# Summing a state-space scan by accumulating DMAs into a channel-major SBUF tile in place of transposes accumulated in PSUM

## The chip, the cores and the metric

The program runs on one core of a Trainium2 chip. Its engines are named as in the profile: PE (TensorE matmul), PEld (its weight loads), DVE (VectorE), ACT (ScalarE), POOL (GpSimd) and SP (SyncE, which here only issues DMAs). The metric is the device time of one execution in microseconds. Three runs of the kernel before gave 1719.56, 1720.71 and 1730.47 us, a median of 1720.71 us. The profiled execution took 1715.39 us, of which 1713.5 us lie between its first and its last instruction (the span).

## The reference

Two layers are computed on an input `x` of shape (2, 2048, 256), float32. The first is a Mamba block with a feed-forward part, multiplied by the SiLU of a second feed-forward part with weights and activations quantized to FP4; the second is an attention over the two batch entries, multiplied by the SiLU of a three-block network with quantized weights. The change touches the Mamba block alone:

```python
xz = x @ in_proj_w
xi, z = jnp.split(xz, 2, axis=-1)                    # 512 channels each
xc = silu(causal_conv4(xi) + conv_b)
dt, Bm, Cm = jnp.split(xc @ x_proj_w, [16, 32], axis=-1)
dt = softplus(dt @ dt_proj_w + dt_proj_b)
A = -jnp.exp(A_log)                                  # (512, 16)
def step(h, inp):
    dt_t, B_t, C_t, x_t = inp
    dA = jnp.exp(dt_t[..., None] * A)
    h = dA * h + dt_t[..., None] * B_t[:, None, :] * x_t[..., None]
    y = jnp.sum(h * C_t[:, None, :], axis=-1)        # the sum over the 16 states
    return (h, y)
y = ys + D * xc
y = y * silu(z)
return y @ out_proj_w
```

## The kernel before

The 2048 positions are cut into 16 units of 128 positions. One unit holds both batch entries, so 256 columns (`T`), and the 512 channels lie as four groups of 128 partitions (`m`). A unit has five stages: HEAD (norm, input projection, convolution, `dt`), QUANT (the FP4 feed-forward), SCAN, TAIL (the feed-forward after the Mamba block) and SECOND (the whole second layer). HEAD of unit u+1 is recorded ahead of the rest of unit u, and SECOND of a unit runs beside the scan of later units.

Nothing is issued where the code stands. A `Recorder` keeps every engine call, and `issue` puts them out in an order that a planner works out beforehand from costs written in `cost`, from data dependences and from free buffers, with hand-set numbers (`lead`, `bonus`, `adjust`, `passes`). The order on each engine's queue is then fixed, and an engine takes its queue strictly in order. All instructions therefore have the helper's line, L579, in the profile, and are told apart by the tiles that they write and read. The pools' buffer counts are fixed too: `hh`, `bcs` and `decay` have two buffers each, `xc` and `ux` one.

The scan (L982 to L1063) goes over the 16 states two at a time, so eight steps per unit and 128 steps in all. For one step:

- SP loads `bcs` (L997): B and C of the two states, copied to all 128 partitions, 512 KB.
- ACT writes `decay`, the exponentials, in eight instructions (L1001), and copies the state carried from the unit before into column 0 of `hh` (L1014).
- DVE multiplies `ux` by B into `hh` (L1017, "the first product"), scans `hh` with `decay` in place (L1019), and multiplies `hh` by C in place (L1027, "the second product"). Each is over 2048 columns.
- SP saves the last column of the scan in `state` (L1023), between the scan and the second product.
- PE transposes the 16 blocks of 128x128 of `hh` and accumulates them in two PSUM banks `y`, position-major (L1031). That is the sum over the states. It begins, per unit, with `D * xc` as eight matmuls against the diagonal `ddiag` (L989).

After eight steps `z` is projected position-major, its SiLU `sz` is multiplied with `y` (L1048), the product is transposed back to channel-major by PE and copied out of PSUM by ACT (L1051, L1053), and eight matmuls with `w_out` give `x2` (L1062). A buffer of `hh` is free for the first product of the next step but one when PE has transposed it.

The eight PSUM banks are shared out in `BANKS` (L30): two for `y`, two for `m` (HEAD and the end of SCAN), two for `f`, one each for `s` and `h`. POOL has little to do: the inverse square roots of the norms (`ln_y`, `ln_sq`, about six per unit).

Of the kernel before, what the change touches and what calls it, by code (L numbers as in the profile page):

```python
# [17 lines left out]
P = 128  # L18
D = 256
# [10 lines left out]
BANKS = {"y": 2, "m": 2, "f": 2, "s": 1, "h": 1}  # L30
USES = {
    "q": "f", "s0": "s", "s1": "s", "h0": "h", "h1": "h",
    "e0": "m", "e1": "y", "g0": "h", "g1": "f",
# [8 lines left out]
class Recorder:  # L42
# [69 lines left out]
    def cost(self, engine, method, args, kwargs):  # L112
# [6 lines left out]
        if engine == "gpsimd":  # L119
            if method == "memset":  # L120
                return 0.04
            return 0.69 if method == "tensor_tensor" else 0.19
# [88 lines left out]
    def prepare(self):  # L211
# [12 lines left out]
        for i, (engine, method, args, kwargs, stage) in enumerate(ops):  # L224
# [14 lines left out]
            if engine == "gpsimd":  # L239
                self.table[i] = int(method != "memset")  # L240
            if engine == "sync":
                self.size[i] = 2 if args[0].dtype == BF16 else 4
                for d in args[0].shape:
                    self.size[i] *= d
# [44 lines left out]
    def backward(self, unit, bonus, ahead):  # L289
# [7 lines left out]
        def transfer(i):  # L297
            return size[i] / self.RATE if engine[i] == "sync" else 0.0
# [68 lines left out]
    def forward(self, key, bonus, ahead):  # L367
# [65 lines left out]
        while done < n:  # L433
# [54 lines left out]
            if best_e == "sync":  # L488

                moved = max(moved, t + cost) + self.size[i] / self.RATE  # L490
                stop = moved + tails["sync"]
# [91 lines left out]
def tile_two_layers(ctx: ExitStack, tc: tile.TileContext, a: dict):  # L583
# [53 lines left out]
    def load_x(u):  # L637
        t = io.tile([P, B, D], F32, tag="xt", name=f"xt_{u}")
        rec.sync.dma_start(t, x[:, u * P : (u + 1) * P, :].rearrange("b p d -> p b d"))
        return t  # L640
# [72 lines left out]
    ddiag = const.tile([P, 4, P], F32, name="ddiag")  # L713
    for m in range(4):
        rec.vector.tensor_scalar(ddiag[:, m, :], ident, dvec[:, m : m + 1], None, ALU.mult)
# [145 lines left out]
    def make_qlora_weights():  # L861

        scl = load("q_scl", [P, 6, 2, D // BLK], a["scales"].rearrange("i (c p) n -> p i c n", p=P))
        wl = const.tile([P, 6, 2, D], F32, tag="w_l", name="w_l")
        for i in range(6):
            qi = tmp.tile([P, 2, D], I32, tag="t2k_s0", name=f"qi_{i}", bufs=depth["s0"])
            rec.sync.dma_start(qi, a["qweights"][i].rearrange("(c p) d -> p c d", p=P))
            lab = t2k("s0", f"lab_{i}")
# [5 lines left out]
            for c in range(2):  # L874
                wv = w[:, c, :].rearrange("p (n k) -> p n k", k=BLK)
                rec.vector.tensor_tensor(
                    wv, wv, scl[:, i, c, :].unsqueeze(2).to_broadcast([P, D // BLK, BLK]), ALU.mult
                )
# [103 lines left out]
    def scan(u, h):  # L982
# [3 lines left out]
        y = [bank("y", f"y_{nm}_{g}") for g in range(TG)]  # L986
        for g in range(TG):
            for m in range(4):
                rec.tensor.matmul(  # L989
                    y[g][:, m * P : (m + 1) * P], lhsT=h["xc"][:, m, g * P : (g + 1) * P],  # L990
                    rhs=ddiag[:, m, :], start=(m == 0), stop=False, skip_group_check=True,
                )
        bcv = h["bc"].rearrange("(s n) t -> s n t", s=2)
        for n in range(0, NS, 2):
# [32 lines left out]
            rec.vector.tensor_tensor(hv[:, :, :P], hv[:, :, 1:], cn, ALU.mult)  # L1027
            for k in range(2):
                for g in range(TG):
                    for m in range(4):  # L1030
                        rec.tensor.matmul(  # L1031
                            y[g][:, m * P : (m + 1) * P],
                            lhsT=hh[:, k, m, g, :P],
                            rhs=ident, is_transpose=True, start=False, stop=(n + k == NS - 1),
                            skip_group_check=True,
                        )

        y2 = [None] * TG
        for g in range(TG):
            pz = bank("m", f"pz_{nm}_{g}")  # L1040
            for c in range(2):
                rec.tensor.matmul(
                    pz, lhsT=h["lnt"][:, c, g * P : (g + 1) * P], rhs=w_in[:, c, DI : 2 * DI],
                    start=(c == 0), stop=(c == 1),
                )
            sz = scn.tile([P, DI], F32, tag="sz", name=f"sz_{nm}_{g}", bufs=1)
            rec.scalar.activation(sz, pz, AF.Silu)
            rec.vector.tensor_tensor(sz, y[g], sz, ALU.mult)  # L1048
            pt = bank("m", f"py_{nm}_{g}").rearrange("p (m t) -> p m t", m=4)
            for m in range(4):  # L1050
                rec.tensor.transpose(pt[:, m, :], sz[:, m * P : (m + 1) * P], ident)  # L1051
            y2[g] = t2k("m", f"y2_{nm}_{g}").rearrange("p (m t) -> p m t", m=4)
            rec.scalar.copy(y2[g], pt)  # L1053
        po = bank("m", f"po_{nm}").rearrange("p (g d) -> p g d", g=TG)
        for g in range(TG):
            for m in range(4):
                rec.tensor.matmul(
                    po[:, g, :], lhsT=y2[g][:, m, :],
# [255 lines left out]
    for u in range(NU):  # L1314
# [9 lines left out]
        x1 = mam.tile([P, B, D], F32, tag="x1", name=f"x1_{u}")  # L1324
        tail(u, h, x2, sgs, x1)
        rec.stage = (u, SECOND)
        if u == 0:
# [6 lines left out]
        (3, 1, 2.23), (9, 3, -0.03), (15, 4, 1.53), (5, 1, -1.64), (13, 0, 0.68), (14, 4, -2.53),  # L1334
        (3, 3, -0.31), (14, 1, 0.96), (6, 2, -0.01), (11, 4, 1.22), (14, 2, 1), (11, 1, 0.05),
        (8, 0, 0.01), (2, 1, -2.41), (13, 1, 2.14), (3, 2, 0.51), (6, 3, 1.05), (0, 1, 1.16),
        (11, 0, -0.47), (5, 3, -1.29), (14, 0, 0.2), (13, 4, -0.85), (7, 2, 0.99), (12, 1, 0.89),
        (13, 3, -0.99), (1, 2, 0.28), (15, 1, 2.77), (14, 3, -1.39), (8, 1, 0.09), (7, 3, -0.25),
        (15, 3, 1.61), (6, 1, 0.87),
    ]  # L1340
    passes = [
        (20.0, 0.3, 0.0, 1.02, 0.1, [
            (9, 4, -0.033), (9, 1, 0.008), (4, 2, "gpsimd", -0.309), (1, 3, "tensor", 0.016),
            (2, 1, "gpsimd", 0.015), (1, 4, "vector", -0.12), (7, 3, "scalar", -0.018),
            (7, 3, "vector", 0.085), (1, 2, "gpsimd", 0.027), (1, 1, "gpsimd", -0.003),
            (9, 4, "gpsimd", 0.128), (11, 1, "vector", -0.088), (3, 4, "gpsimd", -0.076),
            (15, 4, "vector", 0.027), (1, 2, "scalar", -0.075), (8, 0, "vector", 0.016),
            (15, 3, "scalar", -0.469), (7, 3, -0.043), (13, 0, "vector", -0.017),
            (4, 3, "gpsimd", -0.036), (6, 4, 0.029), (8, 2, "vector", 0.849),
            (7, 0, "vector", -0.277), (9, 1, "vector", 0.009), (8, 2, "gpsimd", -0.192),  # L1350
            (1, 3, "gpsimd", -0.014), (0, 0, -0.03), (1, 1, "scalar", -0.005), (15, 2, 0.008),
            (3, 2, "scalar", 0.081), (7, 4, 0.045), (8, 3, 0.119), (2, 0, "tensor", -0.001),
            (11, 4, -0.015), (6, 3, -0.002), (1, 3, "vector", -0.002),
        ]),
        (10.0, 0.5, 0.02, 0.7, 0.1, [
            (11, 1, -0.102), (2, 4, "scalar", 0.011), (5, 4, "vector", -0.034), (15, 4, -0.012),
            (1, 1, "gpsimd", -0.001), (0, 2, "scalar", 0.062), (6, 1, 0.102),
            (15, 3, "tensor", -0.001), (8, 0, "gpsimd", 0.078), (14, 3, "gpsimd", -0.002),
            (2, 3, "gpsimd", 0.073), (15, 0, "vector", 0.003), (11, 4, "gpsimd", -0.513),
            (8, 3, "scalar", 0.034), (6, 2, "vector", -0.182), (1, 0, "tensor", -0.047),  # L1360
            (13, 3, -0.126), (13, 1, "tensor", 0.078), (13, 0, 0.075), (9, 3, "scalar", 0.327),
            (13, 4, "scalar", -0.038), (10, 3, "gpsimd", 0.04), (7, 0, -0.033), (5, 4, -0.02),
            (11, 0, "gpsimd", 0.001), (12, 2, "vector", 0.022), (7, 3, "tensor", 0.011),
            (14, 3, "scalar", -0.562), (5, 1, 0.02), (11, 2, "vector", -0.033),
            (4, 4, "tensor", -0.007), (14, 2, "gpsimd", 0.082), (7, 4, -0.619),
            (12, 4, "gpsimd", -0.108), (0, 0, "vector", 0.038), (7, 0, "gpsimd", 0.595),
            (3, 0, "tensor", -0.063), (10, 1, "gpsimd", -0.034), (10, 3, "scalar", -0.054),
        ]),
        (20.0, 0.3, 0.12, 0.2, 0.12, [
            (11, 0, -0.044), (2, 3, 0.079), (0, 3, "scalar", -0.007), (5, 0, "tensor", 0.001),  # L1370
            (12, 2, "vector", -0.004), (9, 1, "scalar", -0.003), (7, 2, "gpsimd", 0.03),
            (6, 1, "scalar", 0.003), (11, 0, "gpsimd", 0.036), (10, 2, "gpsimd", -0.008),
            (12, 4, "gpsimd", -0.078), (15, 1, "tensor", 0.002), (7, 4, "vector", 0.006),
            (12, 0, -0.001), (10, 4, "tensor", 0.001), (4, 0, "vector", 0.015),
            (1, 0, "scalar", 0.054), (7, 0, -0.019), (12, 0, "gpsimd", 0.131),
            (1, 3, "gpsimd", 0.007), (8, 4, 0.054), (5, 1, "tensor", 0.032),
            (1, 1, "gpsimd", 0.061), (4, 2, "gpsimd", 0.387), (4, 4, -0.231),
            (7, 1, "scalar", 0.028), (12, 2, "gpsimd", 0.017), (8, 1, "tensor", 0.007),
            (8, 0, "tensor", 0.003), (3, 3, -0.006), (13, 0, "tensor", -0.004),
            (2, 3, "gpsimd", -0.063), (3, 4, "scalar", -0.014),  # L1380
        ]),
        (110.0, 0.3, 0.08, 0.206, 0.02, [
# [154 lines left out]
```

## Time and profile before

| | us |
|---|---|
| three runs, median (lowest, highest) | 1720.71 (1719.56, 1730.47) |
| profiled execution, whole | 1715.39 |
| its span, first to last instruction | 1713.5 |
| DVE busy | 1614.3 (94%), 1638 instructions |
| PE busy | 1552.3 (91%) |
| ACT busy | 1419.4 (83%), of it 313 table loads 401.6 |
| POOL busy | 183.5 (11%) |
| DMA engines | 25.5% of 16 engines, 86.36 MB on SP's queue |

The busy times by stretch are read as follows: from 100 to 1600 us DVE stands still for some 26 us in all (it is busy for 1474.0 us of them); the rest of its idle time is at the ends, 11.6 us in the first 100 us and 61.5 us after 1600 us. After 1616 us, when the last second product is over, the last unit's TAIL and SECOND run as one dependent chain that PE carries.

One unit is some 98 us long. Its eight steps take 8 x (2.28 + 4.45 + 2.28) us of DVE by the rows' means, and the rest of DVE's unit is the FP4 quantization, the norms and the gates.

### The profile page before, as it was taken

How to read it: one execution, taken by the hardware profiler on the slowest of the kernel's cores; microseconds unless marked ns; L12 is line 12 of the kernel's file. 1: busy time of each engine (PE TensorE's matmuls, PEld its weight loads, DVE VectorE, ACT ScalarE, POOL GpSimd, SP SyncE). 2: the span in 40 equal slices, each digit the busy share in tenths (PEclk: the TensorE clock that was granted, in tenths of full speed). 3: DMA queues.
4: the chain of work that ended last, by engine and by line, in shares of the span. 5: the costliest groups of instructions: out<-in, count | busy, mean ns of one | idle time of the engine just before them, and what ended most of it. 6: DMA issues, size and time to landing. Idle time of an engine off the chain costs nothing.

```text
span 1713.5 us, 21982 instructions
## 1 busy us (share of the span) xinstructions
PE 1552.3 (91%) x7948; PEld 1224.1 (71%) x7948; DVE 1614.3 (94%) x1638; ACT 1419.4 (83%) x2885; POOL 183.5 (11%) x114
## 2 busy tenths in 40 slices
PE   7736989999899999989999998999989899998997
PEld 5535758678687867768687876878677686867775
DVE  8999999999999999999999999999998999999932
ACT  5636877989899899899989898999978898897734
POOL 0000002001011201020102011001130101100100
PEclk9858989999999999999999999999999999999999
DMA  7322222313222232222222331222222132211000
GB/s 188 92 46 51 50 46 46 61 32 57 57 46 47 47 63 38 44 58 50 53 47 47 57 58 32 51 64 38 57 44 46 44 51 51 51 44 50 25 7 13
DMA packets 310666, 87.75 MB, mean 51 GB/s; under 512 B 262775, under 2 KB 276765, under 8 KB 310558
## 3 DMA queue, kind: packets, MB, share of 16 engines
q1 hardware_dynamic: 310558, 86.36, 25.5%
q8 instruction: 62, 1.02, 0.2%
q14 instruction: 46, 0.38, 0.1%
HBM read 80.62 MB, written 4.72 MB: 50 GB/s over the span
## 4 chain that ended last, share of the span: by engine, by line
PE 41%; ACT 20%; DVE 9%; issue 3%; POOL 1%; DMA 0%; POOLq 0%; ACTq 0%; SPq 0%; DVEq 0%
PE bank_f L579 16%; PE bank_m L579 8%; PE bank_s L579 7%; ACT decay L579 7%; PE bank_y L579 6%; ACT L579 6%; DVE hh L579 4%; ACT t2k_s L579 3%; PE bank_h L579 2%; DVE fp_l L579 2%; ACT t2k_f L579 1%; DVE t2k_s L579 1%; ACT dt L579 1%; POOL ln_sq_s L579 1%; ACT fp_h L579 0%
## 5 line engine op out<-in xcount | busy, mean ns | idle before, releaser
L579 DVE TENSOR_TENSOR_SCAN hh<-decay,hh 128x2064 f32<-128x2064 f32 x128 | 569.7, 4451 | 1.4 <-DVE ln_m_m L579 0.4
L579 ACT ACTIVATE decay<-dt,amat 128x256 f32<-128x256 f32 x1024 | 437.5, 500 | 34.3 <-DVE hh L579 33.0
L579 ACT ACT_TABLE_LOAD x313 | 401.6, 1283 | 16.5 <-DVE hh L579 3.9
L579 PE MATMUL bank_y<-ident,hh 128*128 128x128 f32 x2048 | 279.8, 283 | 36.1 <-DVE hh L579 36.1
L579 PEld LDWEIGHTS bank_y<-ident,hh 128*128 128x128 f32 x2048 | 246.6, 147 | 72.1 <-issue 47.1
L579 DVE TENSOR_TENSOR hh<-ux,bcs 128x2048 f32<-128x2048 f32 x128 | 291.8, 2279 | 6.7 <-PE bank_y L579 6.5
L579 DVE TENSOR_TENSOR hh<-hh,bcs 128x2048 f32<-128x2048 f32 x128 | 291.9, 2281 | 0.1
L579 POOL TENSOR_TENSOR ln_sq_s<-ln_sq_s,power 128x2 f32<-128x2 f32 x45 | 86.9, 1932 | 755.2 <-ACT ln_sq_s L579 755.2
L579 PE MATMUL bank_f<-w_f,t2k_f 128*128 128x256 f32 x512 | 133.6, 388 | 11.4 <-ACT t2k_f L579 11.3
L579 PE MATMUL bank_f<-t2k_f,w_f 128*128 128x256 f32 x512 | 127.6, 389 | 4.0 <-ACT t2k_f L579 3.3
L579 PE MATMUL bank_m<-xi,cdiag 128*128 128x256 f32 x512 | 124.8, 378 | 0.0
L579 PEld LDWEIGHTS bank_f<-w_f,t2k_f 128*128 128x128 f32 x512 | 94.3, 193 | 30.7 <-ACT t2k_f L579 17.6
L579 PEld LDWEIGHTS bank_f<-t2k_f,w_f 128*128 128x128 f32 x512 | 97.8, 194 | 21.7 <-ACT t2k_f L579 6.2
L579 PEld LDWEIGHTS bank_m<-xi,cdiag 128*128 128x128 f32 x512 | 93.6, 189 | 14.2 <-issue 0.5
L579 PE MATMUL bank_h<-t2k_s,w_l 128*128 128x256 f32 x360 | 92.0, 390 | 8.6 <-ACT t2k_s L579 8.6
L579 PE MATMUL bank_f<-w_down,hq 128*128 128x256 f32 x384 | 93.1, 386 | 6.7 <-ACT hq L579 6.5
L579 DVE SCALAR_TENSOR_TENSOR fp_l<-fp_h,fp_l 128x704 f32<-128x704 f32 (+2 forms) x124 | 91.8, 740 | 6.8 <-ACT fp_h L579 6.4
L579 PE MATMUL bank_f<-w_up,t2k_f 128*128 128x352 f32 x256 | 91.4, 475 | 6.0 <-ACT sg L579 2.9
L579 PE MATMUL bank_s<-w_qkv,t2k_s 128*128 128x256 f32 (+1 forms) x300 | 90.8, 430 | 4.1 <-DVE t2k_s L579 4.1
L579 PE MATMUL bank_f<-w_gate,t2k_f 128*128 128x352 f32 x256 | 90.0, 471 | 2.0 <-ACT h L579 2.0
L579 PE MATMUL bank_s<-w_l,t2k_s 128*128 128x256 f32 x360 | 89.3, 381 | 0.6 <-ACT t2k_s L579 0.6
L579 PEld LDWEIGHTS bank_f<-w_down,hq 128*128 128x128 f32 x384 | 71.6, 192 | 22.3 <-ACT hq L579 11.5
(172 smaller groups left out, 2434.2 us busy)
## 6 DMA issues: line engine op xcount, KB each, us to landing
bcs<-bc SPq DMA_DIRECT2D x128, 512.0 KB, 4.9
xt<-in_x_dram SPq DMA_DIRECT2D x16, 256.0 KB, 3.8
out_dram<-t2k_s SPq DMA_DIRECT2D x15, 256.0 KB, 2.2
w_f<-in_ffn_w_dram SPq DMA_DIRECT2D x2, 1024.0 KB
state<-hh SPq DMA_DIRECT2D x120, 8.0 KB, 2.9
t2k_s<-in_qweights_dram SPq DMA_DIRECT2D x6, 256.0 KB, 3.1
w_in<-in_in_proj_w_dram SPq DMA_DIRECT2D x1, 1024.0 KB, 5.1
h<-in_w_gate_dram SPq DMA_DIRECT2D x6, 128.0 KB
```

Of the source, the lines that this page charges most:

```text
L579: getattr(getattr(self.nc, engine), method)(*args, **kwargs)
```

## The change

The diff, with the planner's hand-set numbers (`adjust`, `passes`, `lead`, `bonus`) left out; all of those are new.

```diff
-BANKS = {"y": 2, "m": 2, "f": 2, "s": 1, "h": 1}
+BANKS = {"m": 3, "f": 2, "s": 2, "h": 1}
...
-    "e0": "m", "e1": "y", "g0": "h", "g1": "f",
+    "e0": "m", "e1": "m", "g0": "h", "g1": "f",
...
         if engine == "gpsimd":
+            if method == "dma_start":
+                return 1.1
...
-        t = io.tile([P, B, D], F32, tag="xt", name=f"xt_{u}")
+        t = io.tile([P, B, D], F32, tag="xt", name=f"xt_{u}", bufs=4)
...
-    ddiag = const.tile([P, 4, P], F32, name="ddiag")
-    for m in range(4):
-        rec.vector.tensor_scalar(ddiag[:, m, :], ident, dvec[:, m : m + 1], None, ALU.mult)
...
-        scl = load("q_scl", [P, 6, 2, D // BLK], ...)
         for i in range(6):
...
+            scl = small.tile([P, 2, D // BLK], F32, tag="q_scl", name=f"scl_{i}", bufs=2)
+            rec.sync.dma_start(scl, ...)
...
-        y = [bank("y", f"y_{nm}_{g}") for g in range(TG)]
-        for g in range(TG):
-            for m in range(4):
-                rec.tensor.matmul(
-                    y[g][:, m * P : (m + 1) * P], lhsT=h["xc"][:, m, g * P : (g + 1) * P],
-                    rhs=ddiag[:, m, :], start=(m == 0), stop=False, skip_group_check=True,
-                )
+        y = mam.tile([P, 2, 4, T], F32, tag="y", name=f"y_{nm}", bufs=1)
+        yv = y.rearrange("p k m (b t) -> p (k m b) t", b=B)
+        xc = h["xc"]
+        for m in range(4):
+            rec.scalar.activation(xc[:, m, :], xc[:, m, :], AF.Copy, scale=dvec[:, m : m + 1])
...
-            rec.vector.tensor_tensor(hv[:, :, :P], hv[:, :, 1:], cn, ALU.mult)
-            for k in range(2):
-                for g in range(TG):
-                    for m in range(4):
-                        rec.tensor.matmul(
-                            y[g][:, m * P : (m + 1) * P],
-                            lhsT=hh[:, k, m, g, :P],
-                            rhs=ident, is_transpose=True, start=False, stop=(n + k == NS - 1),
-                            skip_group_check=True,
-                        )
+            if n == 0:
+                rec.vector.tensor_tensor(yv, hv[:, :, 1:], cn, ALU.mult)
+                rec.gpsimd.dma_start(y[:, 0], xc, accum_op=ALU.add)
+            else:
+                rec.vector.tensor_tensor(hv[:, :, :P], hv[:, :, 1:], cn, ALU.mult)
+                rec.gpsimd.dma_start(yv, hv[:, :, :P], accum_op=ALU.add)
+        rec.gpsimd.dma_start(y[:, 0], y[:, 1], accum_op=ALU.add)
...
-            sz = scn.tile([P, DI], F32, tag="sz", name=f"sz_{nm}_{g}", bufs=1)
+            sz = scn.tile([P, 2, T], F32, tag="sz", name=f"sz_{nm}_{pr}", bufs=1)
             rec.scalar.activation(sz, pz, AF.Silu)
-            rec.vector.tensor_tensor(sz, y[g], sz, ALU.mult)
-            pt = bank("m", f"py_{nm}_{g}").rearrange("p (m t) -> p m t", m=4)
-            for m in range(4):
-                rec.tensor.transpose(pt[:, m, :], sz[:, m * P : (m + 1) * P], ident)
-            y2[g] = t2k("m", f"y2_{nm}_{g}").rearrange("p (m t) -> p m t", m=4)
-            rec.scalar.copy(y2[g], pt)
+            half = y[:, 0, 2 * pr : 2 * pr + 2, :]
+            rec.vector.tensor_tensor(half, half, sz, ALU.mult)
...
-                    po[:, g, :], lhsT=y2[g][:, m, :],
+                    po[:, g, :], lhsT=y[:, 0, m, g * P : (g + 1) * P],
...
-        x1 = mam.tile([P, B, D], F32, tag="x1", name=f"x1_{u}")
+        x1 = h["xt"]
```

The sum over the states now lives in one SBUF tile `y`, channel-major, of [128, 2, 4, 256] float32: one half for the even and one for the odd state of a step. The first step's second product writes it directly. POOL then issues a DMA of 512 KB that adds `xc`, scaled by `D` in place by four ACT instructions. Each of the other seven steps adds its 2048 columns of `hh` by a DMA of 1 MB: its source is 16 rows of 128 elements (512 bytes) per partition, with one element between rows, and its destination is contiguous. A last DMA of 512 KB adds the odd half to the even one. So there are nine accumulating DMAs per unit, in all 144, on POOL's queue, and each of them writes bytes that the one before it wrote, so each waits for the landing of the one before. `z` is projected channel-major (eight matmuls of 256 columns per unit for four of 512), the gate multiplies `y` in place, and the `w_out` matmuls take `y` as it lies.

The tile `y` has one buffer. `hh` still has two: a buffer is free for the next step but one when the DMA that reads it has landed. `x1` is now written over `xt`, which gets a fourth buffer, and the scales `q_scl` are loaded in six parts. The two banks of `y` go to `m` and `s`. The planner counts an accumulating DMA at 1.1 us of POOL and its bytes at the same rate as SP's transfers.

## The prediction

> **What bounds the kernel now.** First the page's busy times; then two stretches of the busy times by window (stretch, length, busy us and instructions of PE, PEld, DVE, ACT, POOL, then granted clock, DMA share, GB/s).
>
> ```profile
> PE 1552.3 (91%) x7948; PEld 1224.1 (71%) x7948; DVE 1614.3 (94%) x1638; ACT 1419.4 (83%) x2885; POOL 183.5 (11%) x114
> ```
> ```profile
> 692.00:790.00 98.00, 93.06 (x483) 73.89 (x482) 97.49 (x92) 88.32 (x175) 15.84 (x5) 1.00 0.26 50
> ...
> 1400.00:1600.00 200.00, 186.83 (x966) 147.26 (x964) 197.85 (x174) 175.70 (x364) 16.30 (x11) 0.97 0.24 50
> ```
>
> In a unit of 98 us DVE stands still for 0.5 us. PE is close behind, but DVE cannot be passed: from 100 to 1600 us its idle time is 26 us in all, and that is the most that relieving PE can return there. So the change is worth little if everything it adds is hidden, and the question is what DVE waits for afterwards.
>
> Next, the groups of instructions by form (line, engine, operation, tiles, shapes, count | busy us, mean ns | idle before):
>
> ```profile
> L579 DVE TENSOR_TENSOR_SCAN hh<-decay,hh 128x2064 f32<-128x2064 f32 x128 | 569.7, 4451 | 1.4 <-DVE ln_m_m L579 0.4
> L579 DVE TENSOR_TENSOR hh<-hh,bcs 128x2048 f32<-128x2048 f32 x128 | 291.9, 2281 | 0.1
> L579 DVE TENSOR_TENSOR hh<-ux,bcs 128x2048 f32<-128x2048 f32 x128 | 291.8, 2279 | 6.7 <-PE bank_y L579 6.5
> L579 PE MATMUL bank_y<-ident,hh 128*128 128x128 f32 x2048 | 279.8, 283 | 36.1 <-DVE hh L579 36.1
> ```
>
> A step is 9.0 us of DVE. The first product waits for the freeing of `hh` by PE's transposes only 6.5 us in the whole run: 16 x 0.283 = 4.5 us of transposes fit easily beside the other buffer's step. That is the place where the accumulating DMA will stand.
>
> Last, the DMA issues (queue, count, KB each, us from issue to landing), and POOL's instructions on `power` (shortest/median/longest ns):
>
> ```profile
> bcs<-bc SPq DMA_DIRECT2D x128, 512.0 KB, 4.9
> ...
> state<-hh SPq DMA_DIRECT2D x120, 8.0 KB, 2.9
> ...
> w_in<-in_in_proj_w_dram SPq DMA_DIRECT2D x1, 1024.0 KB, 5.1
> ...
> bc<-xdbl SPq DMA_DIRECT2D x32, 16.0 KB, 1.5
> ```
> ```profile
> L579 POOL TENSOR_TENSOR ln_sq_s<-ln_sq_s,power x45: 692/1765/9580, 271.6 to 1698.1; 128x2 f32<-128x2 f32 x45
> ```
>
> **The change part by part.** PE loses 279.8 (transposes), 38.3 (`ddiag`) and 21.6 us (the transposes of `sz`); `z` costs the same either way (256 records of 394 ns in the same form, 66 us, for 128 of 621 ns, 65.6 us). That leaves 1213 us, 71%. ACT: the order of the changed program has 364 table loads for 313, 51 x 1.283 = +65 us; 64 scalings of `xc`, nearest row `decay` at 500 ns, +32 us; the 32 copies of `y2` go, -18.5 us. It comes to 1498 us, still below DVE. DVE has the same instructions but for four of 0.27 us; the gate reads SBUF in place of PSUM, and rows of 512 elements take 681 ns from either. The larger PSUM shares, `x1` over `xt` and five more small loads at the start touch nothing that is late.
>
> So 26 us can come back in the middle. ACT, which grows by 79 us, causes part of DVE's waits, so I take 10. At the end the last unit's gate follows the last second product through two DMAs instead of transposes: it came 7.5 us after it (1623.2 against 1615.8) and would come some 18 us after. `x2` came only at 1636.7, since PE was taken up by other work, so I take +5 of the 11 us.
>
> *What one DMA costs.* No accumulating DMA and no DMA from POOL is in the trace. From the rows: a 16 KB transfer lands in 1.5 us (the fixed part). `state` moves hardly any bytes but 2048 elements one by one (120 x 2048 of the page's 262775 packets under 512 bytes), as many pieces as the 2048 runs of 512 bytes here, and lands in 2.9 us: 1.4 us for the pieces. 1 MB of `w_in` takes 5.1 - 1.5 = 3.6 us. An adding DMA must fetch its destination as well; I count its bytes twice, 7.2 us. It shares the engines with SP's transfers, 0.255 x 98 / 8 = 3.1 us of engine time per step, and `bcs` is released by the same second product; half of it, 1.5 us, is taken. Landing time of 1 MB: L = 1.5 + 1.4 + 7.2 + 1.5 = 11.6 us; of 512 KB in long runs: 1.5 + 3.6 + 1.5 = 6.6 us. Lower end: the second fetch and SP's share cost nothing, 6.5 us. Upper end: bytes at the rate of `bcs`, (4.9 - 1.5) x 2 = 6.8 us per MB, twice, and all of SP's share: 19.6 us, and 11.4 us for 512 KB. A gain below 6.5 us is excluded by the bytes. I stay at 11.6, since `w_in` is the row of equal size.
>
> *What waits for it.* The order of the changed program on DVE, with the durations of the rows, gives the work between a second product and the reuse of its `hh` buffer. Of 110 such places the shortest are 4.8 (one), 8.6 and 8.8 us, the median is 11.9; shortfalls sum to 6, 21, 50 and 97 us at L = 9, 10, 11 and 12. But the DMAs also wait for one another. From a unit's first `y` product to its gate the order holds 82.6 us of DVE work (mean of units 1 to 14); the chain needs 7 x 11.6 + 2 x 6.6 = 94.4 us. DVE waits the 11.8 us that are missing, chiefly at the first products: 16 x 11.8 = 189 us. ACT's copy of `state` into `hh` waits at the same landings (now for PE, 21.8 us), and behind it in ACT's queue stand the exponentials of later steps. On POOL six powers per unit stand between DMAs and come up to one landing late; SECOND and the next HEAD wait for those, and as both run beside the scan, I cost that at nothing; uncovered it is 96 powers x some 1 to 4 us, within the range's upper part. One buffer of `y` costs nothing: the next unit's product comes some 13 us after the gate, and two products of 0.68 us and 4.0 us of `w_out` matmuls (64.6 / 16) lie between.
>
> Sum: 1715.4 - 10 + 5 + 189 = 1899, say 1900 us. The profiled execution lies 5 us below the median of the runs shown and 4 us below the lowest, so it is a fair base, and 5 us are nothing beside the terms above.
>
> Two rules of the Trainium skill pull opposite ways here. "DMA: Bandwidth & Descriptors", in its anatomy of a DMA issued from GpSimd, fits 2.0 us plus bytes over 436 GB/s; that would be 4.4 us for 1 MB, below the 5.1 us of `w_in`, DVE would never wait, and the sum would be 1694 us. "Collectives: The Full Stack", in the section on the bandwidth ceiling, holds against the change that a reducing transfer reads two sources and so runs at about half the rate of a copy; on `w_in`'s row that is my doubling. No row of this trace decides between them.
>
> **The rivals.**
>
> *Hidden (faster).* If the destination's fetch overlaps the source's, L stays at or below 8.6 us, the shortest reuse but one; DVE never waits and the 26 us of idle time come back: 1715.4 - 26 + 5 = 1694 us. For it: the DMA engines are 25.5% busy, and 2048 pieces cost only 1.4 us. It decides up to L = 8.6.
>
> *Break-even.* L between 8.6 and 9.7 us: shortfalls of 3 to 16 us eat what PE returns, 1703 to 1730 us. A narrow window.
>
> *POOL as the bound (much slower).* The descriptors of a POOL DMA come from POOL itself. Its power of two columns takes 0.69 us alone and up to 9.58 us beside DVE, which never rests. If producing 2048 runs, or getting at memory beside DVE, adds 4 us, L = 15.6 and 512 KB take some 8: 7 x 15.6 + 16 - 82.6 = 42.6 us per unit, 1710 + 682 = 2392 us; at the upper end of the transfer, 7 x 19.6 + 22.8 - 82.6 = 77.4, it is 2948 us. Against it: POOL is 11% busy.
>
> *ACT or PE bound.* At 1498 and 1213 us neither reaches DVE's 1614.
>
> That the change does not do what it says is unlikely: the changed order has no transpose of `hh`, and 144 DMAs on POOL.
>
> **How the numbers follow.** Forecast (L from 9.8 to 13.5, 1735 to 2150 us): 0.50, as it asks only that the second fetch costs something. POOL or a slow transfer, above 2150: 0.20. Hidden: 0.19; its full 26 us need not come back, so a fifth of it ends within 1%. Break-even: 0.11. About 1% is what a measurement of this kernel can tell from no change, 1703 to 1738 us: faster 0.16, same 0.14, slower 0.70. The range goes from 1694 us, which all of DVE's waits returned would give, to 2380 us, L of about 15.5; some 0.13 lie above and 0.05 below. The forecast's own range is 1735 to 2150.
>
> **What would show it.** Right: DVE's first product `hh<-ux,bcs` waits for DMAs of POOL's queue by 150 us or more, DVE's busy time stays at 1610 to 1620 us, PE falls to some 1215, and the `y` DMAs of 1 MB land after 10 to 13 us, one behind the other. Hidden would show landings below 8.6 us and a first product that hardly waits. POOL as the bound would show long spans of POOL before any packet moves, with DMA engines idle between. The prediction is wrong if the landing time is; each us of L is worth 110 to 130 us (16 units, seven landings of 1 MB and two smaller), so that is the number to look at first. ACT waiting in front of `hh<-state` far longer than DVE would make the queue behind it the cause instead.

## The result, and the profile after

| | before | after |
|---|---|---|
| runs, median (lowest, highest), us | 1724.93 (1719.56, 1730.47) | 2024.72 (2024.3, 2034.83) |
| ratio, 95% interval | | 1.175 (1.169 to 1.181) |
| span of the profiled execution, us | 1713.5 | 2022.9 |
| DVE busy / idle within the span, us | 1614.3 / 99.2 | 1628.1 / 394.8 |
| mean granted TensorE clock | 0.963 | 0.838 |

The change costs 300 us. (A time below is the median of the runs at a kernel's usual granted clock; one of the four runs of a later experiment, at 0.623 and 2271.77 us, is left out.) The forecast was 1900 us, its own range 1735 to 2150: the direction and the place were right, and the time was 125 us too low. The span grew by 309.4 us, of which 295.6 are idle time of DVE and 13.8 are busy time, so the question is again what DVE waits for.

The busy times of the page, with the queues of its third part (packets, MB, share of 16 engines' span; q0 is POOL's queue, q1 is SP's):

```profile
PE 1452.6 (72%) x5644; PEld 1070.5 (53%) x5644; DVE 1628.1 (80%) x1634; ACT 1496.8 (74%) x2968; POOL 452.1 (22%) x258
...
q0 software_dynamic: 235776, 134.23, 55.8%
q1 hardware_dynamic: 310638, 86.36, 22.8%
```

Two stretches by window, one unit and the same 200 us as before (columns as in the prediction):

```profile
891.00:1009.00 118.00, 90.75 (x353) 67.68 (x352) 100.28 (x99) 91.50 (x187) 22.66 (x16) 0.86 0.84 111
1400.00:1600.00 200.00, 147.77 (x545) 106.28 (x544) 162.53 (x140) 160.05 (x318) 44.41 (x25) 0.80 0.82 109
```

No engine is full any more: DVE, ACT and PE are busy for 85%, 78% and 77% of a unit, and the unit is 118 us long where it was 98. Such a picture points to a chain across engines. The groups of the page's fifth part and the DMA issues of its sixth name it:

```profile
L581 POOL DMA_DIRECT2D y<-hh x112 | 236.1, 2108 | 849.6 <-DMA y<-hh 234.2
L581 DVE TENSOR_TENSOR hh<-ux,bcs 128x2048 f32<-128x2048 f32 x128 | 292.6, 2286 | 144.7 <-DMA y<-hh 140.6
...
y<-hh POOLq DMA_DIRECT2D x112, 1024.0 KB, 11.4
bcs<-bc SPq DMA_DIRECT2D x128, 512.0 KB, 5.4
y<-xc POOLq DMA_DIRECT2D x16, 512.0 KB, 7.0
y<-y POOLq DMA_DIRECT2D x16, 512.0 KB, 4.6
...
state<-hh SPq DMA_DIRECT2D x120, 8.0 KB, 5.4
```

The first product now waits 140.6 us for the landing of the adding DMAs (it waited 6.5 us for PE), and 1 MB lands in 11.4 us; the prediction had 11.6. What DVE waits for in all, from the view of its waits (engine and tile, what it waited for, us in total, times, longest):

```profile
DVE hh L581 <- DMA y<-hh: 140.6, 57, 9.4
DVE ln_m_m L581 <- POOL ln_y_m L581: 56.6, 7, 13.6
DVE h L581 <- PE bank_f L581: 32.2, 12, 6.4
DVE t2k_f L581 <- PE bank_f L581: 26.6, 7, 18.0
DVE ln_m_f L581 <- POOL ln_y_f L581: 26.4, 7, 6.6
DVE t2k_s L581 <- ACT t2k_s L581: 21.9, 11, 7.0
```

All lines of that view added up by the engine waited for, before and after: DMA 1.1 and 146.7 us, POOL 4.6 and 89.9, PE 60.9 and 93.6, ACT 23.7 and 51.5.

The page's fourth part follows the work that ended last back from releaser to releaser, and gives the engines' shares of the span:

```profile
DMA 36%; ACT 20%; PE 17%; DVE 17%; issue 6%; POOL 3%; SPq 0%; POOLq 0%; ACTq 0%; DVEq 0%
```

The 36% are landings of `y` (before, DMA had 0% there). So the landings lead, but not alone: in between, this chain runs over ACT, PE and DVE for more than half of the span.

The timeline of POOL for the unit from 891 to 1009 us (start, length, instruction, the idle time ahead of it and what ended it) shows the chain link by link, and what stands between the links (a releaser is inferred; ahead of 926.19 it reads ACT, but the second product of DVE that this DMA reads ended only at 925.5):

```profile
892.69 0.86 POOL L581 DMA_DIRECT2D y<-xc  x1 [21.94 <-DVE ln_st_f L581]
900.34 2.12 POOL L581 DMA_DIRECT2D y<-hh  x1 [6.79 <-DMA y<-xc]
901.54 1.65 POOL L581 TENSOR_TENSOR ln_y_f<-ln_y_f,power 128x2 f32<-128x2 f32 x1
902.24 1.94 POOL L581 TENSOR_TENSOR ln_y_m<-ln_y_m,power 128x4 f32<-128x4 f32 x1
912.45 2.15 POOL L581 DMA_DIRECT2D y<-hh  x1 [8.28 <-DMA y<-hh]
926.19 2.09 POOL L581 DMA_DIRECT2D y<-hh  x1 [11.59 <-ACT hh L581]
...
962.87 2.13 POOL L581 DMA_DIRECT2D y<-hh  x1 [5.26 <-DMA y<-hh]
...
974.82 2.13 POOL L581 DMA_DIRECT2D y<-hh  x1 [4.58 <-DVE ln_m_s L581]
986.50 0.89 POOL L581 DMA_DIRECT2D y<-y  x1 [9.56 <-DMA y<-hh]
1005.40 1.08 POOL L581 TENSOR_TENSOR ln_y_f<-ln_y_f,power 128x2 f32<-128x2 f32 x1 [18.00 <-DVE ln_y_f L581]
1009.36 0.89 POOL L581 DMA_DIRECT2D y<-xc  x1 [2.87 <-DVE ln_m_f L581]
```

The second number of a line is POOL's own part of a DMA, about 2.1 us for the large ones. From 962.87 to 974.82 it is 11.95 us, one landing and 0.6 us until the next issue. The two powers at 901.54 and 902.24 could start only when the DMA ahead of them in POOL's queue had been let go by the landing of `xc`; `ln_y_f` and `ln_y_m` are what DVE's norms wait for in the list above. The powers themselves are little longer than before (of `ln_sq_s` the median is 1929 ns where it was 1765, and the longest 5662 where it was 9580).

### The profile page after: what moved, and what is told of

It is laid out like the page before. It is cut to its first block, busy times and chain, and to the rows that moved or that the text cites. A ratio compares the mean times of both kernels' runs of the same rounds, so it can differ in the third digit from the quotient of the medians.

```text
span 2022.9 us, 17770 instructions
## 1 busy us (share of the span) xinstructions
PE 1452.6 (72%) x5644; PEld 1070.5 (53%) x5644; DVE 1628.1 (80%) x1634; ACT 1496.8 (74%) x2968; POOL 452.1 (22%) x258
## 3 DMA queue, kind: packets, MB, share of 16 engines
q0 software_dynamic: 235776, 134.23, 55.8%
## 4 chain that ended last, share of the span: by engine, by line
DMA 36%; ACT 20%; PE 17%; DVE 17%; issue 6%; POOL 3%; SPq 0%; POOLq 0%; ACTq 0%; DVEq 0%
DMA y<-hh 31%; DVE hh L581 8%; PE bank_f L581 8%; ACT L581 6%; ACT decay L581 5%; PE bank_m L581 5%; DMA y<-xc 5%; ACT t2k_s L581 3%; PE bank_s L581 3%; DVE fp_l L581 2%; DVE y L581 2%; PE bank_h L581 1%; POOL y L581 1%; POOL ln_sq_s L581 1%; DVE fp_sc L581 1%
## 5 line engine op out<-in xcount | busy, mean ns | idle before, releaser
L581 ACT ACTIVATE decay<-dt,amat 128x256 f32<-128x256 f32 x1024 | 441.8, 499 | 62.5 <-DVE hh L581 60.9
L581 POOL DMA_DIRECT2D y<-hh x112 | 236.1, 2108 | 849.6 <-DMA y<-hh 234.2
L581 DVE TENSOR_TENSOR hh<-ux,bcs 128x2048 f32<-128x2048 f32 x128 | 292.6, 2286 | 144.7 <-DMA y<-hh 140.6
L581 DVE TENSOR_TENSOR hh<-hh,bcs 128x2048 f32<-128x2048 f32 x112 | 255.4, 2280 | 0.8
L581 PE MATMUL bank_m<-lnt,w_in 128*128 128x256 f32 x512 | 143.5, 425 | 22.5 <-ACT lnt L581 13.2
L581 PE MATMUL bank_f<-ident,fp_l 128*128 128x128 f32 x292 | 59.6, 343 | 136.1 <-DVE fp_l L581 112.8
L581 PE MATMUL bank_s<-ident,t2k_s 128*128 128x128 f32 x348 | 77.4, 333 | 102.1 <-ACT t2k_s L581 87.0
L581 POOL TENSOR_TENSOR ln_sq_s<-ln_sq_s,power 128x2 f32<-128x2 f32 x45 | 112.9, 2508 | 128.0 <-ACT ln_sq_s L581 128.0
L581 PEld LDWEIGHTS bank_m<-lnt,w_in 128*128 128x128 f32 x512 | 104.4, 213 | 50.4 <-ACT lnt L581 14.9
L581 PEld LDWEIGHTS bank_f<-ident,fp_l 128*128 128x128 f32 x292 | 43.2, 173 | 153.1 <-DVE fp_l L581 124.0
L581 PEld LDWEIGHTS bank_s<-ident,t2k_s 128*128 128x128 f32 x348 | 50.2, 172 | 135.3 <-ACT t2k_s L581 102.7
L581 PEld LDWEIGHTS bank_h<-t2k_s,w_l 128*128 128x128 f32 x360 | 80.1, 232 | 57.2 <-ACT t2k_s L581 43.0
## 6 DMA issues: line engine op xcount, KB each, us to landing
y<-hh POOLq DMA_DIRECT2D x112, 1024.0 KB, 11.4
```

What stands on the lines that cost most here:

```text
L581: getattr(getattr(self.nc, engine), method)(*args, **kwargs)
```

## The experiments

Each kernel ran beside the kernel before on its chip; ratios are to that (its median was 1717 to 1721 us beside the experiments, so a few us between two kernels on different chips mean nothing). Where nothing else is said the edit stands in `issue`, behind the planner, so that the order on every engine is that of the changed kernel, and only the edited instructions differ.

**A copy in place of the addition.** All 112 DMAs of 1 MB overwrite `y`; the additions are left out.

```diff
+ if engine == "gpsimd" and method == "dma_start" and len(args[1].shape) == 3 and args[1].shape[1] == 16:
+     kwargs = {}
```

> The 112 DMAs of 1 MB copy hh over y instead of adding it (the sum over the states is left out); the order of all engines and all waits are those of the changed kernel. Theory (the destination's fetch is counted like a second transfer, and the serial chain of landings sets the unit's length): issue to landing falls from 11.4 us by about 3.6 us to some 7.8 us, the chain per unit from 118 us to 118 - 7 x 3.6 = 93 us, below DVE's 97 us of work, so the time falls to 1710 to 1780 us. Rival (the pieces and POOL's issue of 2.1 us make the landing, the second fetch is hidden): landing stays above 10.5 us and the time above 1930 us.

1860.07 us, ratio 1.083 (1.078 to 1.089). From its page:

```profile
q0 software_dynamic: 35072, 134.23, 25.7%
...
L583 DVE TENSOR_TENSOR hh<-ux,bcs 128x2048 f32<-128x2048 f32 x128 | 292.0, 2282 | 12.6 <-DMA y<-hh 12.3
L583 POOL DMA_DIRECT2D y<-hh x112 | 132.0, 1179 | 737.7 <-DVE hh L583 219.9
...
y<-hh POOLq DMA_DIRECT2D x112, 1024.0 KB, 8.0
```

The landing falls to 8.0 us as the theory said, so the addition costs 3.4 us per MB (POOL's own part of a DMA is 0.9 us shorter too, 1.18 for 2.11, and may be in that), and the wait of the first product is all but gone (12.3 us). The time misses both expectations: 165 us go, but 143 stay. The largest part of POOL's wait ahead of these DMAs is now for DVE (219.9 of 737.7 us), so something else holds the kernel there.

**Long runs.** The same bytes and the same addition, but the source is one run of 8 KB per partition for 16 of 512 bytes. It takes in the gaps of `hh`, so the values are shifted.

```diff
- rec.gpsimd.dma_start(yv, hv[:, :, :P], accum_op=ALU.add)
+ rec.gpsimd.dma_start(y.rearrange("p k m t -> p (k m t)"), flat[:, : 2 * 4 * T], accum_op=ALU.add)
```

> The source of each 1 MB DMA is read as one run of 8 KB per partition, starting at column 0 of hh, instead of 16 runs of 512 bytes (so the values added are shifted and include the carried column); bytes, waits and orders as in the changed kernel. Theory: the 2048 pieces cost 1.4 us of the landing, so 10.0 us, POOL's issue falls from 2.1 to 0.9 us (the row of the 512 KB DMAs, which have long runs), and the time by 16 x 7 x 1.4 = 157 us to some 1870 us. Rival (bytes and SP's share make the whole landing): landing within 0.4 us of 11.4, time above 1980 us. Other rival (descriptors make most of it): landing below 8.5 us, time below 1780 us.

1863.46 us, ratio 1.085 (1.079 to 1.092), the time as expected; the landing fell further, to 9.4 us for the 10.0 expected. From its page:

```profile
q0 software_dynamic: 20736, 134.23, 35.6%
...
L581 DVE TENSOR_TENSOR hh<-ux,bcs 128x2048 f32<-128x2048 f32 x128 | 292.2, 2283 | 33.3 <-DMA y<-hh 31.6
...
y<-hh POOLq DMA_DIRECT2D x112, 1024.0 KB, 9.4
```

The short runs cost 2.0 us of the landing. POOL's own part of a DMA falls by 1.2 us with them, from 2.11 to 0.88, and it lies inside the landing; how much of the 2.0 us is that and how much the transfer itself, no run separates. Shortening the landing by 2.0 us returns 161 us, by 3.4 us (the copy) only 165: with this order and the powers on POOL, a landing shorter than 9.4 us returns next to nothing more. The landing, POOL's part included, as the cause of some 160 us is shown by both runs, made in two different ways.

**Without the two small DMAs of a unit.** The addition of `xc` and that of the odd half are left out.

```diff
+ if engine == "gpsimd" and method == "dma_start" and len(args[1].shape) == 3 and args[1].shape[1] == 4:
+     continue
```

> The two 512 KB DMAs of each unit (the addition of xc and of the odd half of y) are left out, so D*xc and the odd states are missing from the output; all else as in the changed kernel. Theory (serial chain): each unit's chain is shorter by 7.0 + 4.6 us of landings and two releases of 0.6 us, 12.8 us, so the time falls by some 205 us to 1820 us, to 1850 at most. Rival (POOL's late powers and the lower PE clock make DVE wait, the chain is only one of several waits): it falls by less than 100 us, to 1930 us or more.

1912.96 us, ratio 1.114 (1.111 to 1.117), between the two expectations. The two links are 7.0 + 4.6 us of landings per unit, 16 x 11.6 = 186 us, and 112 us come back; DVE's first product still waits 86.9 us. They are part of the chain, though not worth their whole length.

**POOL's powers away.** The 96 powers become reciprocals on DVE; the square root is left out of the norms.

```diff
+ if engine == "gpsimd" and method == "tensor_tensor":
+     engine, method, args = "vector", "reciprocal", args[:2]
```

> The 96 powers on POOL are replaced by reciprocals on DVE at the same places of the order (1/v in place of 1/sqrt(v): the root is left out), so that nothing but DMAs and memsets stands in POOL's queue. Theory (serial chain): the 83 us that DVE waits for POOL's powers go, but the chain of landings still sets the unit, so the time stays within 40 us of 2025 us. Rival (the powers held up behind waiting DMAs in POOL's queue are what the prediction left out): it falls by 80 us or more, to 1945 us or less, which would be most of the 125 us by which the forecast was short.

2010.3 us, ratio 1.171 (1.167 to 1.174), as the theory expected; its 95% interval overlaps the changed kernel's. DVE waits for POOL no more, and waits for the DMAs instead, 222.3 us for 140.6:

```profile
DVE hh L583 <- DMA y<-hh: 222.3, 81, 9.2
```

This is how a second-longest wait looks: taken away, its time goes to the longest. The 89.9 us in the list of waits are no price.

**A third buffer of `hh`.** `w_up` lies over `w_gate` and `w_ao` over `w_out` to make room, so values alone differ.

```diff
+ if t["name"] == "hh":
+     u, n = name.split("hh_")[1].split("_")[:2]
+     self.place[name] = (8 * int(u) + int(n) // 2) % 3
+ if t["name"] == "w_up":
+     self.places[t["tag"], 0] = {F32: self.w_gate}
+ if t["name"] == "w_ao":
+     self.places[t["tag"], 0] = {F32: self.w_out}
```

> hh gets a third buffer; the order of every engine is that of the changed kernel. (For its room the up weights of the FP4 part share the tile of the gate weights and w_ao that of w_out, so the output differs there; shapes and counts stay.) Theory (the DMAs of a unit run one behind the other, each 12.0 us after the last, and this chain sets the unit): DVE's waits at the first products shrink, but others grow and the time stays within 30 us of 2025 us. Rival (the two buffers of hh are the limit, as the prediction's list of reuses has it): the 140 us of these waits go and the time falls to 1920 us or less.

2005.06 us, ratio 1.164 (1.158 to 1.170), as expected: the first product waits for a landing for 4.8 us in all, but the powers and PE take its place (`ln_m_m` 65.3 us, `bank_f` 45.7 + 38.8), and a unit is still 117.2 us. The buffers of `hh` alone were not it.

**No DMA of POOL at all.** All 144 are left out, and so is the sum over the states but for the first step.

```diff
+ if engine == "gpsimd" and method == "dma_start":
+     continue
```

> All 144 DMAs on POOL's queue are left out (the output lacks 7 of 8 steps of the sum, D*xc and the odd states); orders of all engines as in the changed kernel. Copying instead of adding and reading one run both ended at some 1860 us although their landings differ by 1.4 us, so something else holds the unit at 107 us. Theory A (powers held up behind DMAs in POOL's queue): without DMAs they are prompt, DVE's waits for POOL fall under 10 us and the time to 1760 us or less. Theory B (PE's lower granted clock, 0.87 against 0.963 before, and ACT's 79 us of added work, in a fixed order): the time stays at 1820 us or more, and DVE waits mostly for PE and ACT.

1802.36 us, ratio 1.047 (1.042 to 1.051), between the two, nearer the second. This run has the prediction's second miss in it: with every new transfer gone and PE relieved, the kernel is 81 us slower than before, not 20 faster. Its waits of DVE:

```profile
DVE t2k_f L583 <- PE bank_f L583: 31.9, 9, 18.7
DVE h L583 <- PE bank_f L583: 26.4, 11, 6.6
DVE hh L583 <- ACT hh L583: 21.3, 19, 4.3
DVE t2k_s L583 <- ACT t2k_s L583: 15.6, 10, 4.1
```

They are spread over PE and ACT, neither of which is full (PE 77%, ACT 83%).

**Long runs and no powers on POOL,** the two edits shown above for them, together.

> The one-run source of e2_onerun and the reciprocals on DVE of e4_recip together (the root left out, the added values shifted). Where the chain is no longer the limit, the powers' place shows: theory A (POOL's queue makes the 1860 us): 1810 us or less. Theory B (PE's clock and ACT): within 20 us of e2_onerun's 1863 us.

1820.72 us, ratio 1.057 (1.053 to 1.062), between the two expectations, nearer the first: 43 us less than with long runs alone. Behind the shorter landing, powers held up in POOL's queue do have a price; behind the long one most of it was covered.

**PE relieved in the kernel before.** Its order stays; of the 16 transposes of a step only two are left (one for each bank), and the sum over the states is left out with the others. (`rank` counts the transposes of a step from 0 to 15.)

```diff
+ if kwargs.get("is_transpose") and self.ops[i][2][0].tensor.name.startswith("y_"):
...
+     if self.rank[i] not in (11, 15):
+         continue
```

> The kernel before, with its order, and 14 of the 16 transposes of hh of each step left out (the last channel group of the second state stays, one for each bank, so that banks and buffers are freed by the same queue); 1792 of 7948 matmuls, 1792 x 0.137 us apart by the row of 0.283 us at most 250 to 500 us of PE, go. The sum over the states is left out with them. It asks whether a relieved PE alone, with its lower granted clock, slows this kernel. Theory C (the clock): the granted clock falls from 0.96 towards 0.88, DVE waits for bank_f more, and the time rises to 1755 to 1800 us. Rival D (the clock costs nothing here): the time stays within 12 us of the kernel before or falls by up to 26 us, DVE's idle time in the middle.

1732.03 us, ratio 1.0074 (1.0053 to 1.0096): between the two, nearer the rival. From its page:

```profile
PE 1413.9 (82%) x6149; PEld 1039.4 (60%) x6156; DVE 1614.2 (93%) x1638; ACT 1417.8 (82%) x2885; POOL 199.2 (12%) x114
```

PE's busy time falls by 138 us, the granted clock from 0.963 to 0.926, and the kernel becomes 14 us slower. Taking work away from PE costs a little time here. The matmuls that stay take longer (`bank_f<-w_f,t2k_f` 400 ns for 388, `bank_h` 412 for 390), and DVE's waits grow by 8.5 us for PE and by 8.8 for ACT; that the clock is the cause fits this, but no run changed the clock alone.

**ACT relieved in the kernel without DMAs.** The scalings of `xc` are left out, and `sz` and `h` use the exponential in place of the SiLU, which spares 48 table loads.

```diff
+ if engine == "gpsimd" and method == "dma_start":
+     continue
...
+ if engine == "scalar" and method == "activation" and logical.startswith("xc_") and "bias" not in kwargs:
+     continue
+ if engine == "scalar" and method == "activation" and args[2] == AF.Silu and logical.startswith(("sz_", "h_")):
+     args = [*args[:2], AF.Exp]
```

> The kernel without any of the 144 DMAs (1802 us), in the same order, with ACT's growth taken back: the 64 scalings of xc are left out (64 x 0.504 = 32 us), and sz and h take the exponential in place of the SiLU, so that the order holds 316 table loads for 364 (48 x 1.283 = 62 us). ACT should be busy for some 1397 us, 22 below the kernel before. Theory A (ACT's growth is what is left): the time falls by 60 us or more, to 1742 us or less. Rival D (the new fixed order and PE's clock): it falls by less than 25 us, to 1777 us or more.

1829.73 us, ratio 1.063 (1.059 to 1.066): 27 us slower, with ACT busy for 1404.1 us where it was 1490.2. In this order, ACT's growth is not what is left. Why less ACT work makes it slower isn't settled; the order was made for the longer one, and DVE's waits grew at several places (`t2k_s` on ACT 28.4 us for 15.6, `h` on ACT 8.4 for 1.8), none of them large.

**Another order without DMAs.** They are taken out before the planner makes the order, and only two of its refining passes are kept.

```diff
 def issue(self, tc, **how):
+    self.ops = [o for o in self.ops if o[:2] != ("gpsimd", "dma_start")]
+    how["passes"] = how["passes"][:2]
```

> The kernel without any of the 144 DMAs again, but the DMAs are taken out before the planner makes the order, and only the first two of its refining passes are kept; the order then holds 344 table loads for 364. The same work as in the kernel without DMAs that kept the changed kernel's order (1802 us), in another order. Theory E (what was left there is the order, made around DMAs that the planner counts at about 9 us each): DVE's idle time in the middle goes and the time falls to 1730 to 1755 us. Rival D (PE's lower clock and the longer ACT work hold it up in any order): 1785 us or more.

1751.92 us, ratio 1.020 (1.017 to 1.022), as theory E expected: 50 of the 81 us go with another order. It also holds 20 table loads fewer, ACT being busy for 1464.6 us where it was 1490.2; in the run above, 86 us less of ACT returned nothing. That the old order lost these 50 us because it was made around the DMAs is argued: the planner's passes differ too.

**The complete kernel, its order made for the DMAs as they are.**

```diff
             if method == "dma_start":
-                return 1.1
+                return 2.1
...
+                if engine == "gpsimd":
+                    self.size[i] *= 1.2
...
+        how["passes"] = how["passes"][:1]
```

> The changed kernel, complete, with the planner's count of an accumulating DMA of 1 MB raised from about 9.2 us (1.1 of POOL, 6.4 of bytes, 1.7 until it is seen) to about 11.4 (2.1, 7.6, 1.7), the landing measured, and the first refining pass alone; so the order is made for the DMAs as they are. Theory E (part of the loss is an order made for shorter DMAs): the landing stays at 11.4 and the time falls from 2025 to 1980 us or less, at best to the sum of the chain, 16 x 114 + some 100 = 1930. Rival F (the chain of landings sets the time in any order): within 30 us of 2025.

2051.59 us, ratio 1.194 (1.190 to 1.197): the rival's side, and no gain. Landings stay at 11.4 us, and a unit takes 119.8. This order did not shorten the chain; it had one refining pass, so a better one isn't excluded.

**The chain cut in two.** Three of a unit's seven large DMAs add into a second tile `y_b`, which is never added to `y`; room as for the third `hh` buffer.

```diff
+ step = int(self.ops[i][2][1].tensor.name.split("hh_")[1].split("_")[1]) // 2
+ if step % 2 == 0:
+     args[0] = self.y_b.rearrange("p k m (b t) -> p (k m b) t", b=2)
```

> The changed kernel with the chain cut in two: the DMAs of three of the seven steps (the third, fifth and seventh step of a unit) add into a second SBUF tile, so that neighbouring DMAs no longer write the same bytes and need not wait for each other's landing. Counts, bytes, runs and order stay; that tile is never added to the sum, so three steps are missing from the output. Room for it comes from letting w_up lie over w_gate and w_ao over w_out (values alone change). Theory (the DMAs wait for one another): the time between two issues falls from 12.0 us to some 9.5, two DMAs are in flight at a time, each lands later (13 to 16 us) since they share engines that were 56% busy with them, and the time falls to 1840 to 1920 us. Rival (the engines' rate or the freeing of hh sets the time, not the mutual wait): 1980 us or more.

1953.77 us, ratio 1.136 (1.131 to 1.141), between the two. The median landing is 11.6 us on `y` and 12.1 on `y_b`, below the 13 to 16 expected, since most of the DMAs overlap for only a little. Where two were issued within 2.5 to 6.3 us of each other (10 of 37 pairs between 300 and 1700 us), the first landed after 12.5 to 14.8 us and the second after 15.1 to 18.1, so they do slow each other. The timeline of its POOL:

```profile
983.40 2.11 POOL L595 DMA_DIRECT2D y<-hh  x1 [7.15 <-DVE fp_l L595]
987.99 2.08 POOL L595 DMA_DIRECT2D y_b<-hh  x1 [2.48 <-DVE t2k_s L595]
...
1006.32 2.14 POOL L595 DMA_DIRECT2D y<-hh  x1 [15.18 <-DVE hh L595]
...
1015.43 2.13 POOL L595 DMA_DIRECT2D y_b<-hh  x1 [2.39 <-DVE hh L595]
```

The DMAs go in pairs, here 4.6 and 9.1 us apart, and then comes a pause: the pair holds both buffers of `hh` until it has landed, and only then can DVE make the next two products (the first product at 996.47 us waited 5.07 us for the DMA of 983.40). Two steps take 23.2 us on the mean (9.56 + 13.68) where they took 25.0. So two loops of nearly the same length stand beside each other: landing after landing on `y`, 12.0 us per step at the least, and landing plus 9.0 us of DVE on one `hh` buffer, 20.6 us for two steps at the least and 23.2 here. Opening either alone returns 71 us (the chain) or 20 us (`hh`); shortening the landing shortens both. Opening both at once wasn't tried; by the close pairs, the landings would then be longer.

No version among these beats the kernel before.

## Why the prediction was right, and where it was short

**The landing: right in its sum, with two of its terms tested.** 11.4 us measured for 11.6. The copy of the same bytes in the same runs lands in 8.0 us, and the prediction's sum without the second fetch is 11.6 - 3.6 = 8.0. The second fetch was put at 3.6 us and measured 3.4, the pieces at 1.4 and measured 2.0. Both measured differences may hold some of POOL's own part of a DMA, which the prediction gave no term of its own. The half of SP's share (1.5 us) was a choice that no run tested, so that the whole came out within 0.2 us is in part luck. The two DMAs of 512 KB were put at 6.6 us each and took 7.0 and 4.6; why two of one size differ so is open.

Neither rule of the Trainium skill gives these by itself. The fit of "DMA: Bandwidth & Descriptors" (anatomy of a DMA issued from GpSimd), 4.4 us for 1 MB, is 3.6 us short of even the copy; the same page's section on why small descriptors are slow says that transfers from SBUF to SBUF don't suffer, where the 512-byte runs cost 2.0 of 11.4 us here, POOL's shorter part included. The halved rate of a reducing transfer in "Collectives: The Full Stack" (bandwidth ceiling) has the right direction: POOL's queue took 0.558 x 2022.9 = 1129 us of the engines with all its DMAs adding and 0.257 x 1855.2 = 477 us with the 112 large ones copying, more than twice, while the landing grew by a factor of 1.43.

**The chain: right in mechanism, mis-sized by 8 us per unit.** This is the term that was too small, and it accounts for the 125 us. The prediction has per unit 7 x 11.6 + 2 x 6.6 = 94.4 us against 82.6 of DVE work, 11.8 missing, so a unit of 98 + 11.8 = 109.8 us; measured are 118.0. Mean intervals between successive DMA issues of POOL in the changed kernel, from 300 to 1700 us:

| from, to | us | so per unit |
|---|---|---|
| `xc` to first `hh` | 7.48 | 7.5 |
| `hh` to `hh` (median 12.09) | 12.50 | 6 x 12.50 = 75.0 |
| last `hh` to the fold (the addition of the odd half) | 11.82 | 11.8 |
| landing of the fold | 4.6 | 4.6 |
| chain | | 98.9 |

The landings alone are 7 x 11.4 + 7.0 + 4.6 = 91.4 us. The prediction joined them end to end. Between a landing and the next issue there are some 0.6 us at the least, and 7.5 in all over eight gaps, the rest because POOL or DVE came later; the chain is 4.5 us longer than put. And the chain is not the whole way from a unit's first `y` product to its gate: 0.8 us pass between the end of that product and the issue of `xc`, and 4.0 between the landing of the fold and the gate (means of units 1 to 14 in DVE's timeline), in which DVE is busy with other work of its order; the gate itself waited for the fold only 2.2 us in the whole run. So this way takes 98.9 + 0.8 + 4.0 = 103.7 us for the 94.4 put, DVE is busy for 83.6 of them for the 82.6 put, and 20.1 us are idle where 11.8 were forecast. That is 8.3 us per unit, 16 times 133. In the rest of a unit, 14.4 us for the 98 - 82.6 = 15.4 put, DVE is idle for 0.7 us, hardly ever, as the prediction had it.

**Where the wait shows: partly.** The first products were to wait 189 us, with 150 as the least sign, and wait 140.6; the rest of the chain's delay stands at the norms behind POOL's powers (83.0 us) and at `bank_f`. ACT waited 90.9 us for these DMAs in front of `hh<-state`, less than DVE, so the sign named for a queue behind ACT did not show. With the powers gone it is 222.3 us at the first products. POOL's powers "at nothing" was right for this kernel, but not for a shorter landing: 14 us, within the intervals, with the landing at 11.4, and 43 with 9.4.

**The price of a microsecond of landing: not reached.** 110 to 130 us were put. From 11.4 to 9.4 us it is 161 / 2.0 = 81 us on the mean, and from 9.4 to 8.0 next to nothing (1863 and 1860). The price near 11.4 us may be as put, if the landing stops deciding somewhere above 9.4; no run lies between.

**"The middle gives 10 us back": wrong, though hidden.** The prediction let the rest of the kernel be the old one, with PE relieved. Without any DMA it is at 1802, so the rest alone costs 81 us instead of returning 5 to 20. About 50 of these go with another order; 14 are what a relieved PE cost the kernel before, in its own order; some 20 are left unexplained. How much of the 81 us adds to the 118 us of a unit with the chain isn't known: some may stand in the gaps of the chain above. But the rival "hidden" would have failed by them: a landing of 8.0 us, below its bound of 8.6, gave 1860 and not 1694.

**PE and ACT.** PE was put at 1213 us and is busy for 1452.6: the same matmul of 256 columns takes 425 ns for 388 (`bank_f<-w_f,t2k_f`), 465 for 390 (`bank_h`), beside a granted clock of 0.838 for 0.963. That a relieved PE has slower matmuls was not in the prediction. "TensorE: Matmul & The Clock Gate" (Part 1, on the clock gate) says that activity releases the throttle and idle windows bring it back, which agrees with 0.963, 0.926 and 0.838 at 91, 82 and 72% busy. ACT was put at 1498 us and took 1496.8, and is not the bound, as was said.

**The losing rivals.** POOL as the bound: its issue of a DMA took a steady 2.1 us beside a busy DVE, far from the 4 us more that the rival needed; the landing of 11.4 us includes it.

Read as one sequence of runs (in another sequence the parts may differ), the 300 us are: 161 that go when the runs are long (2025 to 1863), 43 for the powers behind what remains (to 1821), 18 for all the rest of the DMAs, with the powers back on POOL (to 1802), 50 for another order (to 1752), and 34 that are left, 14 of which the relieved PE may account for.

## What to carry to other kernels

Transfers that add into the same bytes form a chain: price it per unit as the number of links times landing plus the gap to the next issue, add what the order puts between the chain's two ends and the work that starts and uses it, and hold that against the work beside it; a bound on what one landing may last isn't enough. Where two loops (here the sum and the buffer) have nearly the same length, an experiment on either alone returns only a part (71 and 20 us here), and one that shortens what both share returns more (161). And work taken away from an engine in an order laid down beforehand may be worth nothing of itself: time the kernel without the new work as well.

## What the runs showed of the hardware

- Adding in place of copying 1 MB from SBUF to SBUF in runs of 512 bytes takes 11.4 us for 8.0, 235776 packets for 35072 on the queue, and 2.11 us of POOL per DMA for 1.18. In one run of 8 KB per partition the addition takes 9.4 us, 20736 packets and 0.88 us of POOL.
- The small `state` transfers beside them, 2048 single elements, land after 5.4 us where they took 2.9. Beside copies with the same short runs they land after 2.9 us again, and beside additions in one run of 8 KB after 3.1.
- Two additions of 1 MB into different tiles, issued within 2.5 to 6.3 us of each other, land after 12.5 to 14.8 us (the first) and 15.1 to 18.1 (the second), where one behind the other takes 11.4 each.
- Taking 138 us of busy time from PE lowered its granted clock from 0.963 to 0.926 and made the kernel 0.7% slower (0.5 to 1.0%).
